# Seven block products in place of eight in a graph layer's polynomial, with an order of issue found by a search

## The chip, the cores and the metric

The kernel runs on one core of a Trainium2 chip. The metric is the device time of one execution in microseconds (us); the number used is the median of the runs. The engines are named as in the profile: PE does matrix products, PEld is its loading of the stationary operand, DVE is the vector engine, ACT the scalar engine, POOL is GpSimd, and SP issues every DMA of this kernel.

## The reference

64 graphs of 256 nodes with 128 features each go through four layers, every one with a residual sum and a layer norm over the features. All graphs share one weighted adjacency matrix A (256 x 256). The first layer is a gated recurrent update that runs five times; it makes most of the products. The second and third are convolution and attention layers. The last layer, which is the one changed, takes three powers of the adjacency over two copies of the same graph:

```
h1 = A @ x;  h2 = A @ h1;  h3 = A @ h2                    # per graph
y  = x@v0 + h1@v1 + h2@v2 + h3@v3 + h1@v4 + h2@v5 + h3@v6  # v: 128 x 128
out = layernorm(x + y)
```

With `q = A x` this is `P + A^2 R`, where `P = x (v0 + I) + q (v1 + v4)` and `R = x (v2 + v5) + q (v3 + v6)`. The weights are centred beforehand, so that the norm has no mean to subtract.

## The kernel before, in words

Two graphs make a pair, and the 32 pairs go through the layers independently of one another, several at a time. All data are 32-bit floats, and a tile is 128 partitions by 512 columns: 2 graphs x 2 blocks of 128 nodes x 128 features.

No engine's order is written by hand. Each piece of work is recorded as an `Op` by `S.add` with the engines that it could run on, an assumed duration for each, and what it reads and writes. When all is recorded, `Schedule.order` (L132) plans: it takes, again and again, the operation that can start earliest by its assumed durations, with the more urgent one first where two can start together (`due`, L128, and what remains of the pair behind it). It also chooses the engine where there is a choice, and a buffer of the class that the value belongs to (`CLASSES`, L41: 30 buffers of class `A` in SBUF, 8 of `PS`, the PSUM banks). The planned starts then give the order in which each engine's instructions are issued. On the chip each engine follows its list in that order and waits wherever an operand or a buffer isn't ready.

Names that matter below: `mm` (L59) is the assumed duration of a product; `MARGIN` makes the assumed durations of all engines but PE 10% longer; `SEEN` and `LAG` are the assumed time until another engine can use a result. `evacuate` (L234) copies from PSUM to SBUF, on ACT or on DVE; its records have the lines 236 and 237. `turn` (L514) transposes a tile: a transpose of 32 x 32 blocks on DVE (L529), one DMA to DRAM (L531), four DMAs back (L537). `spread7` (L553, products at L566) multiplies by an adjacency matrix with seven block products, `spread` (L548) with eight. `products` (L721) multiplies by one or two 128 x 128 matrices. `scale_norm` (L672) takes the mean square on ACT (L645) or DVE, its root on POOL (L650, L653), and scales on ACT or DVE (L665, L667).

`layer3` (L814) of a pair takes `xT`, the turned tile, and `qT = (A x)^T`. Its eight products (L827, L828), each 256 columns wide, give P and R of both graphs at once; R is copied to SBUF (`rr`, two copies of 256 columns), and four products of 256 columns with `a2T` (L835) add A² R to P in PSUM:

```
pr = t.at(2, 2, D)[:, :, b, :]
nc.tensor.matmul(pr, tokens(xT)[:, c, :], vx.ap, start=(b == 0), stop=False, skip_group_check=True)
nc.tensor.matmul(pr, tokens(qT)[:, c, :], vq.ap, start=False, stop=(b == 1), skip_group_check=True)
```

Of the kernel before, what the change touches and what calls it, by code (L numbers as in the profile page):

```python
# [12 lines left out]
P = 128  # L13
N = 256
# [9 lines left out]
SEVEN = {"q1": 4, "g": 4, "q3": 4}  # L24
FIRST, FINAL = 2, 0

# [14 lines left out]
CLASSES = {"X": (512, 15), "T": (512, 4), "A": (512, 30), "H": (520, 6), "B": (1024, 6), "S": (32, 64), "PS": (512, 8), "D": (512, 4), "E": (1024, 8)}  # L41
# [15 lines left out]


def mm(cols):  # L59

    return cols * 0.00168 + 0.005


class Value:
# [3 lines left out]
    def __init__(self, cls=None, ap=None, name="v"):  # L68
        self.cls, self.ap, self.name = cls, ap, name
        self.writers, self.readers, self.left, self.end = [], [], 0, 0.0  # L70


        self.seeded = self.full = False
# [21 lines left out]
class Op:  # L95
    def __init__(self, pair, ways, reads, writes, number, dma):
        self.pair, self.ways, self.reads, self.writes, self.number, self.dma = pair, ways, reads, writes, number, dma
        self.seen = LAG + (sum(dma) if dma else SEEN[ways[0][0].rstrip("+-")])
        self.before, self.then, self.waits, self.ready, self.rest = {}, [], 0, 0.0, 0.0


class Schedule:
# [29 lines left out]
    def order(self, tiles):  # L132
        for op in self.ops:
            op.waits = len(op.before)
            for b in op.before:
                b.then.append(op)
            for v in op.holds:
                v.left += 1
        for op in reversed(self.ops):
            us = min(w[1] for w in op.ways) + op.seen  # L140
            op.rest = us + max((x.rest for x in op.then if x.pair == op.pair), default=0.0)
        free = {cls: [(0.0, t) for t in ts] for cls, ts in tiles.items()}
        full = {}
        engines = dict.fromkeys([*SEEN, "PORT"], 0.0)
        ready = [op for op in self.ops if not op.waits]
        out, moved = [], 0.0
        while ready:
            best = None
            for op in ready:
                held = 0.0  # L150
                for v in op.holds:
                    if v.cls and v.ap is None:
                        held = max(held, min((t for t, a in free[v.cls] if full.get(id(a)) or not v.seeded), default=1e9))
                if held == 1e9:
                    continue
                way = None
                for engine, us, fn in op.ways:
                    us = us if engine == "PE" else us * MARGIN
                    start = max(op.ready, held, *(engines[e] for e in USES.get(engine, (engine,))))
                    end = start + us + SPARE.get(engine, 0.0)  # L160
                    if way is None or end < way[0]:
                        way = end, start, op, engine, us, fn
                late = self.due(op.pair) - op.rest + HOLD[op.layer] if op.pair >= 0 else -1e4
                key = (way[1], late, op.number)
                if best is None or key < best[0]:
                    best = key, *way[1:]
            if best is None:
                raise RuntimeError("no operation can start: too few tiles")
            _, start, op, engine, us, fn = best
            ready.remove(op)  # L170
            for v in op.holds:
                if v.cls and v.ap is None:
                    slot = min((s for s in free[v.cls] if full.get(id(s[1])) or not v.seeded), key=lambda s: s[0])
                    free[v.cls].remove(slot)
                    v.ap = slot[1]
            end = start + us
            engines.update(dict.fromkeys(USES.get(engine, (engine,)), end))
            if op.dma:
                wait, move, seen = op.dma
                moved = max(moved, end + wait) + move * MARGIN  # L180
                op.seen = moved + seen - end + LAG
            out.append((start, op.number, op, fn))
            for v in op.holds:
                v.left -= 1
                v.end = max(v.end, end + op.seen)
                if not v.left and v.cls:
                    free[v.cls].append((v.end, v.ap))
                    full[id(v.ap)] = v.full or v.seeded
            for x in op.then:
                x.waits -= 1  # L190
                same = engine != "SP" and x.ways[0][0].rstrip("+-") == engine.rstrip("+-")
                x.ready = max(x.ready, end + (AGAIN.get(engine.rstrip("+-"), 0.0) if same else op.seen))
                if not x.waits:
                    ready.append(x)

            op.tiles = {v: v.ap for v in op.holds}
        assert len(out) == len(self.ops), "operations that wait for one another"
        self.span = max(engines.values())
        return [(op, fn) for _, _, op, fn in sorted(out, key=lambda x: x[:2])]


@with_exitstack
def kernel(ctx: ExitStack, tc: tile.TileContext, x, xT, adj, adjT, mats, cols, rows, out):
# [11 lines left out]
    def pe(us, fn, r, w):  # L215
        S.add([("PE", us, fn)], r, w)
# [4 lines left out]
    def dve(us, fn, r, w):  # L221
        S.add([("DVE", us, fn)], r, w)
# [144 lines left out]
    pe(mm(256), edge_cols, [rowb, numb], [t1])  # L367
# [20 lines left out]
    pe(mm(1024), edge_values, [erow, colk], [t3])  # L388
# [70 lines left out]
    pe(mm(1024), square, [a, aT], [t7])  # L459
# [17 lines left out]
    centre(vq, lambda: vq.ap, 2)  # L477

# [24 lines left out]
    def tokens(v):  # L503
        return v.at(4, D)
# [37 lines left out]
    def spread(i, right):  # L542

        t = bank()
        for b in range(2):
# [4 lines left out]
            pe(mm(512), fn, [i, right, *[t] * b], [t])  # L550
# [126 lines left out]
    def layer0(x0, hT):  # L677
        h = x0
        for s in range(STEPS):
# [6 lines left out]
            pe(mm(1024), reset, [Wg, w4, hT, mT], [t])  # L686
# [14 lines left out]
            pe(mm(1024), candidate, [w5, u5h, mT, r], [t])  # L701
# [13 lines left out]
    def products(lefts, rights, t=None):  # L715

        first, t = t is None, t or bank()
        for c in range(4):
# [4 lines left out]
            pe(mm(128 * len(lefts)), fn, [*lefts, W1, *[t] * bool(c or not first)], [t])  # L723
        return t

    def layer1(x1):
        qT = spread7(x1, offT, offT7) if S.pair < n_pairs - SEVEN["q1"] else to_sbuf(spread(x1, offT), "qT")
# [14 lines left out]
    def layer2(x2):  # L742
# [3 lines left out]
        for b in range(2):  # L746
# [5 lines left out]
            pe(mm(260), fn, [xT, wpx], [t])  # L752
# [34 lines left out]
        for b in range(2):  # L787
# [6 lines left out]
            pe(mm(512), fn, [wT, h, *[t] * b], [t])  # L794
# [18 lines left out]

    def layer3(x3, p):  # L814
        xT = turn(x3, "xT", "x3")
        qT = spread7(x3, aT, aT7) if S.pair < n_pairs - SEVEN["q3"] else to_sbuf(spread(x3, aT), "qT")

        rr, o = Value("A", name="rr"), Value("A", name="o")
        ts = []
        for i in range(2):  # L820
# [8 lines left out]
            pe(mm(1024), fn, [xT, qT, vx, vq], [t])  # L829
            evacuate(lambda i=i: rr.at(2, N)[:, i], lambda t=t: t.at(512)[:, N:], [t], [rr], (0.28, 0.34))  # L830
            ts.append(t)
        for i, t in enumerate(ts):
# [4 lines left out]
            pe(mm(512), fn, [a2T, rr, t], [t])  # L837
        s, rs = scale_stats([(t, range(i, 4, 2)) for i, t in enumerate(ts)])
        for i, t in enumerate(ts):
            scale_tokens(t, o, range(i, 4, 2), s, rs)  # L840
        S.add([("SP", 0.4, lambda: nc.sync.dma_start(out[2 * p:2 * p + 2].rearrange("b (t p) d -> p (b t) d", p=P), tokens(o)))],
              [o], [], (0.6, 1.0, 0.9))
# [14 lines left out]
    with tc.manual_schedule():  # L857
        for op, fn in S.order(tiles):
            for v, ap in op.tiles.items():
                v.ap = ap  # L860
            fn()
# [40 lines left out]
```

## Time and profile before

| | us |
|---|---|
| median of three runs | 1489.29 |
| lowest and highest run | 1488.52, 1491.57 |
| span of the profiled execution, first to last instruction | 1485.2 |
| median less span (launch and end, and what differs from run to run) | 4.1 |
| PE busy | 1474.5 (99% of the span) |
| DVE busy | 1234.4 (83%) |
| ACT busy | 1026.9 (69%) |
| POOL busy | 829.8 (56%) |
| weight loads busy | 1062.6 (72%) |
| share of the DMA queue's packets of 16 engines' span | 70.7% |

The device time of the profiled execution is not given apart; its span is what the sums are made against, and the 4.1 us are put on top. A record's duration on PE overlaps with the next record's, so the row of PE's busy time only says where PE had nothing at all. A 32-bit product leaves two records of PE in the profile (7704 records are 3852 products).

### The profile page before, as it was taken

The numbers are of one execution on the slowest core, as the hardware profiler recorded it, in microseconds if no ns is written. First come the engines' busy times: TensorE is split into PE (matmuls) and PEld (weight loads), VectorE is DVE, ScalarE is ACT, GpSimd is POOL, SyncE is SP. The second block draws the span as 40 slices with busy tenths as digits, with TensorE's granted clock in tenths as the row PEclk, the third lists the DMA queues.
The fourth block names the chain that finished last, engine by engine and source line by source line (L and its number), as shares of the span: only waits on it lengthen the run. The fifth ranks groups of instructions, "written<-read, shape, count | busy, mean of one in ns | idle before, by whom it ended". The sixth has DMA issues, their size and how long they took to land.

```text
span 1485.2 us, 28119 instructions
## 1 busy us (share of the span) xinstructions
PE 1474.5 (99%) x7704; PEld 1062.6 (72%) x7704; DVE 1234.4 (83%) x3083; ACT 1026.9 (69%) x3116; POOL 829.8 (56%) x1307
## 2 busy tenths in 40 slices
PE   9999999999999999999999999999999999999998
PEld 6556666666676677777767777777676776788997
DVE  7767888988999899888888888878888888989872
ACT  3444556667777787876776767676686767878875
POOL 4412434555576776564556556565454746676542
PEclk9999999999999999999999999999999999999999
DMA  8544565777788978776778668777777776667762
GB/s 239 121 85 99 104 131 121 144 148 152 156 156 173 176 167 171 161 160 135 148 148 178 134 134 174 155 158 143 142 166 148 151 153 124 136 136 148 165 123 71
DMA packets 946845, 216.60 MB, mean 146 GB/s; under 512 B 726017, under 2 KB 942209, under 8 KB 946689
## 3 DMA queue, kind: packets, MB, share of 16 engines
q1 hardware_dynamic: 946688, 214.81, 70.7%
q8 instruction: 62, 1.02, 0.3%
q14 instruction: 95, 0.77, 0.2%
HBM read 116.86 MB, written 97.85 MB: 145 GB/s over the span
## 4 chain that ended last, share of the span: by engine, by line
PE 95%; DVE 2%; DMA 1%; ACT 0%; issue 0%; SPq 0%; POOL 0%; POOLq 0%; ACTq 0%; DVEq 0%
PE ps L566 23%; PE ps L699 9%; PE ps L700 9%; PE ps L684 9%; PE ps L685 9%; PE ps L692 9%; PE ps L721 7%; PE ps L835 4%; PE ps L828 4%; PE ps L827 4%; PE ps L791 4%; PE ps L548 2%; PE ps L751 2%; DMA x<-x_in 1%; DMA a<-e 0%; DVE a L529 0%
## 5 line engine op out<-in xcount | busy, mean ns | idle before, releaser
L566 PEld LDWEIGHTS ps<-aT,a 128*128 128x128 f32 x2144 | 291.4, 192 | 83.3 <-issue 76.7
L236 ACT COPY a<-ps 128x128 f32<-128x128 f32 (+2 forms) x553 | 230.4, 433 | 137.8 <-PE ps L566 48.6
L566 PE MATMUL ps<-aT,a 128*128 128x128 f32 x2144 | 315.7, 275 | 0.9 <-DMA a<-e 0.5
L585 POOL TENSOR_TENSOR a<-a 128x128 f32<-128x128 f32 x205 | 103.7, 510 | 150.4 <-DVE a L581 110.6
L688 ACT ACTIVATE a<-ps,bzrh 128x512 f32<-128x512 f32 x160 | 110.0, 688 | 104.4 <-PE ps L685 90.7
L703 ACT ACTIVATE ps<-ps,bzrh 128x512 f32<-128x512 f32 x160 | 106.1, 663 | 105.3 <-PE ps L700 102.3
L699 PE MATMUL ps<-a,w 128*128 128x512 f32 x320 | 163.7, 593 | 0.0
L685 PE MATMUL ps<-a,w 128*128 128x512 f32 x320 | 163.4, 592 | 0.0
L700 PE MATMUL ps<-a,u5h 128*128 128x512 f32 x320 | 163.4, 592 | 0.0
L692 PE MATMUL ps<-a,w 128*128 128x512 f32 x320 | 162.8, 593 | 0.0
L645 ACT ACTIVATE a<-ps 128x128 f32<-128x128 f32 x488 | 128.7, 282 | 45.9 <-PE ps L721 20.9
L529 DVE STREAM_TRANSPOSE a<-a 128x512 f32<-128x512 f32 x215 | 149.7, 700 | 10.9 <-DMA e<-a 2.2
L587 DVE TENSOR_TENSOR a<-ps,a 128x256 f32<-128x256 f32 x234 | 96.5, 416 | 67.8 <-ACT a L236 32.0
L721 PE MATMUL ps<-W,a 128*128 128x128 f32 x1024 | 144.5, 275 | 0.0
L721 PEld LDWEIGHTS ps<-W,a 128*128 128x128 f32 x1024 | 132.8, 192 | 16.1 <-issue 13.9
L653 POOL TENSOR_TENSOR s<-s,neg_half 128x4 f32<-128x4 f32 x128 | 138.1, 1079 | 7.6
L694 ACT ACTIVATE a<-ps,bzrh 128x512 f32<-128x512 f32 x160 | 110.5, 691 | 45.2 <-PE ps L692 37.8
L684 PE MATMUL ps<-a,W 128*128 128x512 f32 x256 | 131.0, 593 | 0.0
L685 PEld LDWEIGHTS ps<-a,w 128*128 128x128 f32 x320 | 60.8, 190 | 76.5 <-issue 68.1
L700 PEld LDWEIGHTS ps<-a,u5h 128*128 128x128 f32 x320 | 60.8, 190 | 76.5 <-issue 64.8
L705 DVE SCALAR_TENSOR_TENSOR ps<-a,ps 128x512 f32<-128x512 f32 x160 | 109.7, 686 | 6.1 <-ACT a L694 4.4
L573 POOL TENSOR_TENSOR a<-a,a 128x128 f32<-128x128 f32 x133 | 67.3, 507 | 83.6 <-DVE a L572 55.3
(208 smaller groups left out, 3329.2 us busy)
## 6 DMA issues: line engine op xcount, KB each, us to landing
e<-a SPq DMA_DIRECT2D x277, 256.0 KB
a<-e SPq DMA_DIRECT2D x1108, 64.0 KB
e<-b SPq DMA_DIRECT2D x32, 512.0 KB
b<-e SPq DMA_DIRECT2D x128, 128.0 KB
x<-x_in SPq DMA_DIRECT2D x32, 256.0 KB
t<-xT_in SPq DMA_DIRECT2D x32, 256.0 KB
a<-d SPq DMA_DIRECT2D x32, 256.0 KB
y_out<-a SPq DMA_DIRECT2D x32, 256.0 KB
```

Source lines behind the costliest of these rows:

```text
L236: S.add([("ACT", us[0], lambda: nc.scalar.copy(o(), i())), ("DVE", us[1], lambda: nc.vector.tensor_copy(o(), i()))], r, w)
L529: dve(n / 512 * 0.55 + 0.09, lambda: nc.vector.transpose(st.at(n), i.at(n)), [i], [st])
L566: pe(mm(128), lambda: nc.tensor.matmul(blk(t, k), left(), rt(), start=start, stop=True, skip_group_check=True), [*r, right, terms, *[t] * ...
L645: nc.scalar.activation(tokens(junk)[:, c, :], v.at(len(tiles), D)[:, k, :], AF.Square, scale=D ** -0.5, accum_out=mv()[:, c, 1:2])
L653: pool(1.02, lambda: nc.gpsimd.tensor_tensor(rs(), rs(), neg_half.ap, op=ALU.pow), [s, neg_half], [s])
L684: nc.tensor.matmul(t.at(512), mat("u3"), hT.at(512), start=True, stop=False)
L685: nc.tensor.matmul(t.at(512), w4.ap, mT.at(512), start=False, stop=True)
L692: pe(mm(512), lambda t=t, mT=mT: nc.tensor.matmul(t.at(512), w3.ap, mT.at(512), start=False, stop=True, skip_group_check=True), [w3, mT, t ...
L694: act(0.59, lambda t=t, z=z: nc.scalar.activation(z.at(512), t.at(512), AF.Tanh, bias=bzrh.ap[:, 0:1], scale=0.5), [t, bzrh], [z])
L699: nc.tensor.matmul(t.at(512), w5.ap, mT.at(512), start=True, stop=False)
L700: nc.tensor.matmul(t.at(512), u5h.ap, r.at(512), start=False, stop=True)
L721: nc.tensor.matmul(tokens(t)[:, c, :], tokens(i)[:, c, :], w(), start=(first and k == c == 0), stop=(k == len(lefts) - 1), skip_group_chec ...
```

## The change

1. **Layer 3 of pairs 0 to 29.** With the two graphs as rows and x, q as columns, P and R are a 2 x 2 block product: `[[x0, q0], [x1, q1]]` by `[[vx0, vx1], [vq0, vq1]]`. `polynomial7` makes it from seven block products of 2 x 128 columns, with sums of operands ahead of them (on DVE or POOL) and sums of results behind them (on DVE, out of PSUM), as Strassen's scheme in Winograd's form does. The sums of weights (`vt`) are made once, at the start. The last two pairs keep the old form.
2. **The planner.** `order` now keeps up to four plans at a time. Every 60 us of planned time each is continued eight times, once as it is and seven times with the urgency of each operation moved by up to 2 us at random (from a fixed seed); the four with the least idle time of PE are kept, where idle time is counted by a second reckoning that follows each engine in its order with the assumed durations but without the 10%, plus 0.3 of the idle time in the plan itself.
3. **Assumed durations and buffers.** `mm` counts products one by one (0.2241 us for up to 130 columns), and class `A` has 38 buffers. `layer1b` is another form of the second layer; with `L1 = -1` no pair takes it.

```diff
-SEVEN = {"q1": 4, "g": 4, "q3": 4}
+SEVEN = {"q1": 4, "g": 4, "q3": 4, "pr": 2}
+L1 = -1
...
-CLASSES = {"X": (512, 15), "T": (512, 4), "A": (512, 30), ...
+CLASSES = {"X": (512, 15), "T": (512, 4), "A": (512, 38), ...
...
+SOON = {"PE": 0.2, "ACT": 0.17, "DVE": 0.15, "POOL": 0.15, "SP": 0.0}
+WINDOW, TRIES, KEPT, NUDGE, IDLE = 60.0, 8, 4, 2.0, 0.3
-def mm(cols):
-    return cols * 0.00168 + 0.005
+def mm(cols, n=1):
+    return n * (0.2241 if cols <= 130 else cols * 0.001665 + 0.0065)
...
+                late = op.late
+                if seed and op.pair >= 0:
+                    late += NUDGE * ((op.number * 7919 + seed * 104729) * 2654435761 % 4294967296 / 2147483648.0 - 1.0)
                 key = (way[1], late, op.number)
...
+        tracks, until, seed = [self.prepare(tiles)], 0.0, 0
+        while any(t.ready for t in tracks):
+            until += WINDOW
+            found = []
+            for t in tracks:
+                for k in range(TRIES if t.ready else 1):
+                    c = t.copy()
+                    seed += 1
+                    self.run(c, until, seed * bool(k))
+                    found.append(c)
+            tracks = sorted(found, key=lambda t: t.real_idle + IDLE * t.idle)[:KEPT]
+        best = min((t for t in tracks if t.number == len(self.ops)), key=lambda t: t.end)
...
+    vt = fixed([4, D], "vt")
+    for k, (left, right) in enumerate(((lambda: vx.ap[:, 1, :], lambda: vx.ap[:, 0, :]),
+                                       (lambda: vq.ap[:, 1, :], lambda: vt.ap[:, 0, :]),
+                                       (lambda: vq.ap[:, 1, :], lambda: vx.ap[:, 1, :]),
+                                       (lambda: vq.ap[:, 0, :], lambda: vt.ap[:, 1, :]))):
+        dve(0.25, lambda k=k, left=left, right=right: nc.vector.tensor_sub(vt.ap[:, k, :], left(), right()), [vx, vq, vt], [vt])
...
     def layer3(x3, p):
         xT = turn(x3, "xT", "x3")
         qT = spread7(x3, aT, aT7) if S.pair < n_pairs - SEVEN["q3"] else to_sbuf(spread(x3, aT), "qT")
+        if S.pair < n_pairs - SEVEN["pr"]:
+            return polynomial7(xT, qT, p)
...
+    def polynomial7(xT, qT, p):
+
+        half = lambda v, k: v.at(2, N)[:, k]
+        s13, s24, sv, rr, o = (Value("A", name=n) for n in ("s13", "s24", "sv", "rr", "o"))
+        s1, s3, s2, s4 = Part(s13), Part(s13), Part(s24), Part(s24)
...
+        sum_(0.335, 0.8, lambda e: e.tensor_sub(S3(), x0(), x1()), [xT], [s3])
+        sum_(0.335, 0.8, lambda e: e.tensor_sub(S2(), q1(), S3()), [qT, s3], [s2])
+        sum_(0.335, 0.8, lambda e: e.tensor_add(S1(), x1(), q1()), [xT, qT], [s1])
+        sum_(0.335, 0.8, lambda e: e.tensor_sub(S4(), q0(), S2()), [qT, s2], [s4])
+
+        y, t = bank(), Value("PS", name="ps")
+
+        def product(v, k, left, right, r, start=False):
+            def fn():
+                for i in range(2):
+                    nc.tensor.matmul(tokens(v)[:, 2 * k + i, :], left()[:, i * P:(i + 1) * P], right(), start=start and i == 0,
+                                     stop=True, skip_group_check=True)
+            pe(mm(128, 2), fn, [*r, vx, vq, vt, *[v] * (not start)], [v])
...
+        product(y, 0, x0, VX(0), [xT, s2], start=True)
+        product(y, 1, S2, VT(1), [s2])
+        product(t, 0, S1, VT(0), [s1], start=True)
+        evacuate(lambda: half(sv, 0), lambda: half(y, 0), [y], [sv], (0.28, 0.335))
+        dve(0.335, lambda: nc.vector.tensor_add(half(y, 1), half(y, 1), half(sv, 0)), [y, sv], [y])
+        evacuate(lambda: half(sv, 1), lambda: half(y, 1), [y], [sv], (0.28, 0.335))
+        product(y, 1, S3, VT(2), [s3])
+        product(y, 0, q0, VQ(0), [qT])
+        evacuate(lambda: half(sv, 0), lambda: half(y, 1), [y], [sv], (0.28, 0.335))
+        product(y, 1, q1, VT(3), [qT])
+        dve(0.335, lambda: nc.vector.tensor_add(R(1), blocks(t, 0), blocks(sv, 0)), [t, sv], [rr])
+        product(t, 0, S4, VQ(1), [s4])
+        dve(0.335, lambda: nc.vector.tensor_add(R(0), blocks(t, 0), blocks(sv, 1)), [t, sv], [rr])
+        for i in range(2):
+            def fn(i=i):
+                for j in range(2):
+                    nc.tensor.matmul(y.at(2, 2, D)[:, :, i, :], a2T.ap[:, j, i * P:(i + 1) * P], rr.at(2, 2, D)[:, j],
+                                     start=False, stop=(j == 1), skip_group_check=True)
+            pe(mm(256, 2), fn, [a2T, rr, y], [y])
+        scale_norm(y, o)
+        store(o, p)
```

The products of the new form are named below by what stands on their left: x0, S2 and S1 first, then S3 and q0, then q1 and S4, then the four with `a2T`. Because the planner decides anew, hardly any instruction keeps its place: the built order differs from the first few dozen products on.

## The prediction

> **What bounds the kernel now.** I read the page first (busy time, clock, the chain that ended last).
>
> ```profile
> span 1485.2 us, 28119 instructions
> PE 1474.5 (99%) x7704; PEld 1062.6 (72%) x7704; DVE 1234.4 (83%) x3083; ACT 1026.9 (69%) x3116; POOL 829.8 (56%) x1307
> ...
> PEclk9999999999999999999999999999999999999999
> ...
> PE 95%; DVE 2%; DMA 1%; ACT 0%; issue 0%; SPq 0%; POOL 0%; POOLq 0%; ACTq 0%; DVEq 0%
> ```
>
> PE lacks work for 10.7 us of 1485.2, the clock is full, and the chain is 95% PE. A busy row alone proves little, since its records overlap; so next the chain in order of time around 710 us (start, us, what), which shows the pace at which PE gets through products:
>
> ```profile
> 709.82 1.34 PE ps L566 x12
> 711.16 0.45 PE ps L751 x4
> 711.61 0.22 PE ps L566 x2
> 711.83 0.89 PE ps L791 x8
> ...
> 715.14 0.43 PE ps L827 x2
> 715.58 0.43 PE ps L828 x2
> 716.01 0.43 PE ps L827 x2
> 716.44 0.43 PE ps L828 x2
> 716.87 0.67 PE ps L566 x6
> ```
>
> Two records are one product. One of 128 columns takes 1.34/6 = 0.2235 us, whatever its line; four of 256 take 716.87 - 715.14 = 1.73, so 0.4325 each. There is no gap: PE is fed at its own pace. Where it isn't, stretches of the span tell (from:to, length, PE busy and the others):
>
> ```profile
> 0.00:50.00 50.00, 48.59 (x190) 31.07 (x191) 37.31 (x94) 19.73 (x33) 28.03 (x54) 1.00 0.84 220
> 50.00:450.00 400.00, 400.00 (x1860) 257.93 (x1859) 333.41 (x728) 248.24 (x633) 183.58 (x296) 1.00 0.64 128
> 450.00:500.00 50.00, 47.94 (x272) 34.32 (x271) 45.22 (x118) 36.37 (x109) 33.84 (x53) 1.00 0.93 177
> 500.00:1000.00 500.00, 500.00 (x2698) 364.60 (x2699) 425.70 (x1074) 366.84 (x1140) 306.10 (x483) 1.00 0.76 156
> 1000.00:1360.00 360.00, 360.00 (x1985) 267.89 (x1984) 312.58 (x809) 263.52 (x833) 217.87 (x338) 1.00 0.72 145
> 1360.00:1400.00 40.00, 39.01 (x269) 36.19 (x269) 37.21 (x130) 34.82 (x139) 26.73 (x36) 1.00 0.78 160
> 1400.00:1485.00 85.00, 78.93 (x442) 70.56 (x440) 42.93 (x136) 57.34 (x234) 33.62 (x51) 0.99 0.51 106
> ```
>
> The start loses 1.4 us, 450 to 500 loses 2.06 (DMA share 0.93; PE waits for an input tile, a turned tile and a copy), 1360 to 1400 loses 0.99 (on DVE's sum of the second residual), and nothing elsewhere until the end, where 6 us follow the last product: square, root, scaling, store.
>
> [...] the products at L566 have a mean record of 275 ns while records start 112 ns apart. [...] two narrow products cost 0.447 against 0.4325 for a wide one. [...]
>
> **The change part by part**, against the profiled span.
>
> *Products.* Per pair, 8 of 256 columns go (8 x 0.4325 = 3.46) and 14 of 128 come (14 x 0.2235 = 3.13). The products with `a2T` stay four of 256. 30 x 0.33 = **-9.9 us**, all on the path. With PE saturated, work taken from it shortens the span unless something else makes PE wait.
>
> *Side work.* In the built order DVE gets 90 more sums out of PSUM (x 0.416, L587) and 57 of the 120 operand sums (x 0.434); 63 go to POOL (x 0.746). ACT makes 29 more copies of 256 columns (x 0.376, L236). The planner in turn gives POOL 17 of DVE's 512-wide operations (0.7 us each) and ACT 16 of its scalings. So DVE +38 us (about 86%), ACT +24 (71%), POOL +68 (61%). Cost nothing, hidden under PE, as long as each result is early enough. The four sums for `vt` (4 x 0.28 on DVE at the start) lie hundreds of us ahead of their use. No DMA is added or taken away.
>
> *New hand-offs.* Here PE could come to wait. From the tail, where the last `qT` was late: PE's product ends, 0.26 us later ACT begins its copy, and PE goes on 0.05 after it. So q1, which needs a copy after S3 and q0, needs 0.26 + 0.38 + 0.05 = 0.69 us; S3, behind copy, sum and copy, 0.26 + 0.38 + 0.1 + 0.42 + 0.1 + 0.38 + 0.05 = 1.7; `a2T`, behind S4 and a sum, 0.73. I laid the built PE order out at the paces above. The PE work that lies between: before q1 at least 1.12 us, median 2.2, with six pairs under 1.4; before S3 at least 2.45, median 6; before `a2T` 1.3 or more, but for pair 23 (0.45) and pair 29 (none). So only pair 23 waits (0.3 us), and pair 29 (0.73, in the tail). An ACT operation of 0.69 us caught in front of q1's copy would use up the smallest spares.
>
> *The order elsewhere.* The plan is chosen by PE's reckoned idle time, so the two stalls of the middle (3.05 us) may go; their kind (DMA crowding, late sums near the end) may come back elsewhere, and 8 more buffers of class `A` don't speed any transfer. I take two thirds, **-2.0 us**; the bounds are -3.05 (nothing lost) and +6, twice as much again as now.
>
> *The tail.* The last residual tile must be normed and turned before the last pair's products. Before:
>
> ```profile
> 1464.81 0.37 SPq L531 DMA_DIRECT2D e<-a  x1
> 1467.16 1.92 SPq L537 DMA_DIRECT2D a<-e  x4
> ```
>
> The last product of layer 2 (L721) ended at about 1459.4, SP issued the first leg at 1464.81, and the second leg from 1467.16; it has landed at about 1470.6, if the last of its four takes about the 1.5 us (estimate, from the 2.35 of the four times larger first leg). That is 11.2 us, and 13.6 us of products covered it. In the new order there lie between the last L721 product and the use: two block products (0.89), four `a2T` (1.73), eight of the old form (3.46), four L548 (1.73), four old `a2T` (1.73): 9.55 us. The wait is about 1.7 us, pair 29's inside it; DVE and SP have nothing late in front. Before, the tail lost 0.3 there to a copy that the new order covers: **+1.4**. The old form's last pair and what follows its last product stay.
>
> Sum: -9.9 - 2.0 + 0.3 + 1.4 = -10.2, span 1475.0, and with the 4.1 us between span and median **1479.1**.
>
> **The rivals.**
>
> *A, as summed*: 1479.1, own range 1475.5 to 1482. For it: PE without a gap over 1260 us, distances longer than the hand-offs. Chance 0.68.
>
> *B, small waits at the new hand-offs*, or DMA crowding as at 450 to 500: if each copy or sum stands behind one 0.69 us activation, q1 needs 1.38 and S3 3.8; against the distances, pair by pair, this costs 0.5 + 2.6 us; with the middle's stalls unchanged (+2.0) the time is 1484. For it: ACT and DVE are above 70% and issue strictly in order. Against: the old form's copies stood under the same load and PE waited 0.3 us in all for them. Chance 0.20.
>
> *C, slower: DVE or ACT becomes the bound of layer 3.* Hand-offs repeat three times per pair where there was one. If every link stands behind two activations (1.4 us), q1 needs 2.1 and S3 5.9 us; summed over the pairs' distances 6 + 21 = 27 us, so 1506. It turns the sign once waits eat 10.2 us, 0.34 per pair, and is measurably slower at 0.44. Against it: DVE would stand at 86% and has slack in every stretch (426 of 500). Chance 0.05.
>
> *D, the change doesn't take work from PE*: were the narrow products paced at 0.247 us or more (3.46/14), the gain would be nil, and the time 1489.3 - 2.0 + 1.7 = 1489. L566, L721 and L791 all show 0.2235 at such lengths. Chance 0.02. The remaining 0.05 is for an order so much better (all stalls and the tail's wait gone: 1485.2 - 9.9 - 3.4 + 4.1 = 1476, or less where the row hid stalls) or a disturbed figure.
>
> **How the numbers follow.** The prediction is A's. The range 1475 to 1484.5 holds A, the better order's upper half and most of B: a little over 8 in 10. A measurement of this kernel tells 0.2% (3 us) from no change. Faster by more (under 1486.3): A, nine tenths of B, and nearly all of the better order, 0.88. Within: the rest of B, D and the upper foot of A, 0.07. Slower: C, 0.05.
>
> **What would show it.** PE's records rise to 8064 (180 more products, but narrow ones), while PE's busy time falls with the span to about 1464.5, at 99%; the block products start 0.22 us apart. DVE rises to about 86%, ACT to 71%, POOL to 61%. In the list of PE's waits a line for `xT` coming back by DMA, 1 to 2 us, stands at about 1460 us, or the wait on DVE's sum just ahead of it. Wrong would be: PE waits for ACT's copies or DVE's sums inside layer 3 of over 3 us in total (B or C), stretches of the middle with PE below 99% (another order's stalls), or block products further apart than 0.23 us (D).

## The result, and the profile after

The changed kernel takes 1486.14 us (median of four runs, 1485.48 to 1486.72), beside 1488.90 for the kernel before (four runs): a ratio of 0.9986, interval 0.9971 to 1.0001. A later comparison, with twelve runs of the changed kernel, gave 0.9996 (0.9987 to 1.0004). So the change moves the time by nothing that can be told, where 10 us were forecast, and the figure lies outside the forecast's range.

The page of the kernel after, with the shares of the chain that ended last:

```profile
span 1484.7 us, 28833 instructions
PE 1468.3 (99%) x8064; PEld 1066.6 (72%) x8064; DVE 1270.5 (86%) x3182; ACT 1044.6 (70%) x3185; POOL 899.5 (61%) x1383
...
PE 92%; DVE 5%; DMA 1%; ACT 1%; issue 1%; SPq 0%; POOL 0%; POOLq 0%; ACTq 0%; DVEq 0%
```

The counts and shares are the forecast ones to a point: 8064 records, DVE 86%, ACT 70, POOL 61. But PE was busy for 1468.3 us where 1464.5 were expected, and DVE's part of the chain went from 2% to 5%. The stretches of the kernel after (from:to, length, then busy time of PE, weight loads, DVE, ACT, POOL with their records, PE's granted clock, DMA share, GB/s), cut as before:

```profile
0.00:50.00 50.00, 48.80 (x200) 32.15 (x201) 40.17 (x99) 20.68 (x34) 26.52 (x52) 1.00 0.78 209
50.00:450.00 400.00, 400.00 (x1843) 256.56 (x1842) 332.30 (x725) 247.75 (x617) 193.00 (x307) 1.00 0.65 130
450.00:500.00 50.00, 49.60 (x316) 38.79 (x315) 46.05 (x129) 39.87 (x134) 34.93 (x57) 1.00 0.85 169
500.00:1000.00 500.00, 496.99 (x2792) 362.05 (x2791) 441.51 (x1105) 369.17 (x1141) 328.83 (x505) 1.00 0.77 155
1000.00:1360.00 360.00, 359.54 (x2119) 271.65 (x2118) 321.14 (x844) 274.14 (x886) 246.58 (x369) 1.00 0.75 149
1360.00:1400.00 40.00, 38.64 (x310) 37.20 (x309) 37.59 (x130) 34.48 (x136) 33.06 (x47) 1.00 0.71 147
1400.00:1485.00 85.00, 74.74 (x495) 68.18 (x494) 51.77 (x156) 58.51 (x242) 36.58 (x51) 0.99 0.47 100
```

PE lacks 3.0 us between 500 and 1000 (before: nothing), and in the last 85 us it is busy for 74.74 where it was busy for 78.93, though the span is only half a microsecond shorter. PE's list of waits (in us: total, times, longest) names them:

```profile
PE ps L660 <- DMA x<-x_in: 2.5, 1, 2.5
PE ps L1017 <- DVE a L1013: 1.9, 2, 1.5
...
PE ps L994 <- DVE a L1011: 1.0, 1, 1.0
...
PE ps L957 <- DMA a<-e: 0.2, 1, 0.2
```

The first is for an input tile, at 500 us. The next two are for the new sums of results (L1011, L1013), all after 1400 us, and the last is for the turned tile of the last pair. There is no line of L994 behind a copy on ACT.

**One reckoning for all runs.** Busy time hides what is lost when records overlap (a record of L994 lasts 275 ns in the mean, and the next starts 112 ns after it), so I added up PE's records by their starts. At PE's own pace records lie 112, 216 or 429 ns apart, by width (128, 256, 512 columns); the sum of that is the *pace*, and what a start lies later than its pace is *lost*. Every profiled span is, within 0.1 us, 1.2 (before the first product) + pace + lost + 6.3 (behind the last one's start; 6.6 without the search and 6.8 with DVE handicapped). Before: 1.2 + 1470.8 + 6.9 + 6.3 = 1485.2. After: 1.2 + 1461.2 + 16.0 + 6.3 = 1484.7. PE's work fell by 9.6 us, and lost time rose by 9.1.

| kernel | median us | ratio to before | pace | lost | to 450 | 450-560 | 560-1300 | 1300-1425 | then |
|---|---|---|---|---|---|---|---|---|---|
| before | 1486.5-1488.9 | 1 | 1470.8 | 6.9 | 1.7 | 3.3 | -0.6 | 1.7 | 0.8 |
| after | 1486.14 | 0.9986 | 1461.2 | 16.0 | 1.8 | 5.8 | -0.3 | 5.9 | 2.8 |
| after, again | 1486.28 | 0.9996 | 1461.2 | 13.6 | 1.7 | 3.6 | -0.4 | 6.1 | 2.7 |
| no search | 1491.55 | 1.0031 | 1461.2 | 21.6 | 2.6 | 7.6 | 2.2 | 7.0 | 2.2 |
| old products | 1485.74 | 0.9993 | 1470.8 | 4.5 | 2.6 | -0.1 | -0.2 | 2.0 | 0.2 |
| other seed | 1485.22 | 0.9990 | 1461.2 | 18.2 | 2.1 | 2.4 | -0.4 | 11.1 | 3.1 |
| no sums of results | 1482.60 | 0.9977 | 1461.2 | 14.1 | 2.6 | 5.5 | -0.2 | 3.5 | 2.7 |
| no sums of operands | 1482.00 | 0.9970 | 1461.2 | 10.7 | 2.4 | 2.2 | -0.8 | 4.0 | 2.8 |
| no sums | 1480.60 | 0.9961 | 1461.2 | 10.5 | 2.4 | 2.9 | -1.0 | 3.4 | 2.8 |
| load only | 1494.34 | 1.0048 | 1470.8 | 14.7 | 2.8 | 5.3 | 1.1 | 5.3 | 0.3 |
| last 12 pairs old | 1486.21 | 1.0000 | 1464.4 | 10.2 | 2.3 | 3.1 | 0.7 | 3.4 | 0.7 |
| new form in pairs 20-29 only | 1486.06 | 0.9994 | 1467.6 | 11.6 | 1.7 | 1.9 | -0.2 | 5.6 | 2.6 |
| 17 input buffers | 1489.30 | 1.0022 | 1461.2 | 16.5 | 1.8 | -0.1 | 1.3 | 10.8 | 2.7 |
| layer 3 sooner | 1506.43 | 1.0131 | 1461.2 | 37.0 | 2.1 | 0.6 | 4.6 | 12.2 | 17.5 |
| operand sums on POOL | 1490.46 | 1.0024 | 1461.2 | 18.5 | 1.9 | 3.0 | 1.5 | 9.2 | 2.9 |
| the same, last 12 pairs old | 1485.27 | 0.9990 | 1464.4 | 13.0 | 2.0 | 3.4 | 4.7 | 2.7 | 0.2 |
| DVE handicapped | 1495.13 | 1.0064 | 1461.2 | 24.1 | 3.9 | 1.2 | -0.4 | 15.0 | 4.5 |
| DVE handicapped, last 12 pairs old | 1492.16 | 1.0042 | 1464.4 | 17.8 | 3.7 | 1.5 | 0.9 | 10.8 | 1.0 |
| 17 input buffers, last 12 old | 1488.88 | 1.0016 | 1464.4 | 16.9 | 2.7 | -0.1 | 0.0 | 12.1 | 2.2 |
| the same, other seed | 1483.75 | 0.9981 | 1464.4 | 10.7 | 2.3 | 0.2 | -0.5 | 6.8 | 2.0 |

The lost columns are of one profiled execution each (two for the changed kernel, which differ by 2.2 us at 450 to 560). The medians are of several, so the two agree to 2 or 3 us only. The profiles of the other seed (1488.63 us) and of the new form in pairs 20 to 29 (1488.59) are the slowest of twelve runs, that of the last 12 pairs old (1483.86) is the fastest of twelve: their lost time stands 3.4 and 2.5 us too high, and 2.4 too low. The lost time also holds stretches at half of the full clock (last section). In "after" it is one of 3.4 us, at 500 us, which cost 1.7 us, and the mean granted clock of the profiled execution is 0.998. It is 0.998 without the search too, with the other seed (0.97 from 1375 to 1400 us, 0.96 from 1400 to 1425), without the sums of results (0.98 from 450 to 560) and in the second row with DVE handicapped: an estimated one stretch each, as 1.7 us are 0.001 of the span. It is 0.997 in the first of these rows (0.93 from 1350 to 1400) and in the first of the last two rows (0.93 from 1300 to 1350), an estimated two, 0.996 in "layer 3 sooner", an estimated three, and 0.999 or 1.000 in all others. In every later comparison the time of before was 1486.5 to 1486.7, and the ratio is the number to compare by.

### The profile page after: what moved, and what is told of

The parts are those of the page before. It is cut to its first block, busy times and chain, and to the rows that moved or that the text cites. A ratio compares the mean times of both kernels' runs of the same rounds, so it can differ in the third digit from the quotient of the medians.

```text
span 1484.7 us, 28833 instructions
## 1 busy us (share of the span) xinstructions
PE 1468.3 (99%) x8064; PEld 1066.6 (72%) x8064; DVE 1270.5 (86%) x3182; ACT 1044.6 (70%) x3185; POOL 899.5 (61%) x1383
## 3 DMA queue, kind: packets, MB, share of 16 engines
q1 hardware_dynamic: 946688, 214.81, 71.4%
## 4 chain that ended last, share of the span: by engine, by line
PE 92%; DVE 5%; DMA 1%; ACT 1%; issue 1%; SPq 0%; POOL 0%; POOLq 0%; ACTq 0%; DVEq 0%
PE ps L660 23%; PE ps L778 9%; PE ps L779 9%; PE ps L786 9%; PE ps L793 9%; PE ps L794 9%; PE ps L815 7%; PE ps L994 5%; PE ps L915 4%; PE ps L1017 3%; PE ps L642 2%; PE ps L875 2%; DMA x<-x_in 1%; DVE a L623 0%; DVE x L711 0%
## 5 line engine op out<-in xcount | busy, mean ns | idle before, releaser
L324 ACT COPY a<-ps 128x512 f32<-128x512 f32 (+2 forms) x588 | 243.0, 433 | 112.7 <-PE ps L660 41.3
L815 PEld LDWEIGHTS ps<-W,a 128*128 128x128 f32 x1024 | 131.4, 192 | 15.7 <-issue 13.6
L675 POOL TENSOR_TENSOR a<-a 128x256 f32<-128x256 f32 x114 | 84.9, 746 | 88.2 <-ACT a L324 85.9
```

The lines of the kernel that those rows point to most:

```text
L324: S.add([("ACT", us[0], lambda: nc.scalar.copy(o(), i())), ("DVE", us[1], lambda: nc.vector.tensor_copy(o(), i()))], r, w)
L815: nc.tensor.matmul(tokens(t)[:, c, :], tokens(i)[:, c, :], w(), start=(first and k == c == 0), stop=(k == len(lefts) - 1), skip_group_chec ...
```

## The experiments

All edits are to the changed kernel, and "the search" is the planner's. Only the three runs that leave sums out keep PE's order. Every other run but the repeat has an order of its own, and two orders of the same work differ by up to 5.1 us (the last two rows), which is more than most differences below. Theory D is throughout that the load of the side work, on DVE above all, gives the saving back; its rivals are told in the expectations that name them.

### The two halves of the change apart

```diff
-WINDOW, TRIES, KEPT, NUDGE, IDLE = 60.0, 8, 4, 2.0, 0.3
+WINDOW, TRIES, KEPT, NUDGE, IDLE = 60.0, 1, 1, 2.0, 0.3     # no search
...
-SEVEN = {"q1": 4, "g": 4, "q3": 4, "pr": 2}
+SEVEN = {"q1": 4, "g": 4, "q3": 4, "pr": 32}                # old products
...
-        tracks, until, seed = [self.prepare(tiles)], 0.0, 0
+        tracks, until, seed = [self.prepare(tiles)], 0.0, 5000   # other seed
```

> The changed kernel with the planner's search taken out (one plan, one continuation, no nudges); seven products, new assumed durations and 38 buffers stay. Theory 1 (the new hand-offs cost time where few pairs are left, at the end): PE loses 5 to 7 us beyond its pace after 1360 us as in the changed kernel, with waits on the sums of layer 3; time 1486 to 1490. Theory 2 (the stalls belong to the one order that the search found): the end loses 2 us or less, and the time is 1480 to 1484.

> The search, the assumed durations and the buffers of the change, but layer 3 with eight products in all 32 pairs. Theory 1: the end's losses fall back to about 2 us as before the change; the middle's stall at the first reloaded input may stay; time 1487 to 1490 (before's, less what the search wins). Theory 2: losses at the end of 5 us or more although no new hand-off is there; time 1492 or more.

> The changed kernel with another start of the random numbers in the search: another order of the same work. Theory 1: the same time to 1 us (1485 to 1487), and 5 us or more lost after 1360 us. Theory 2: a time that differs by 3 us or more in either direction, the losses at other places.

> The changed kernel again, unaltered, so that it stands beside the others on their chip. Both theories: 2 to 3 us under the kernel before.

Measured: without the search the new products are slower than before, 1.0031 (1.0018 to 1.0044). The search with the old products is at 0.9993 (0.9984 to 1.0002): it removes 2.4 us of lost time (3.4 at 450 to 560, less 1 elsewhere), about what I had forecast for it. Another seed gives 0.9990 (0.9982 to 0.9999), with 11.1 us lost at 1300 to 1425. So neither half, nor both, brings what the fewer products save; and the loss moves with the order. The expectations missed in size: without the search the time is above the 1486 to 1490 us of theory 1, with the old products it is below its 1487 to 1490, and the changed kernel was 0.2 us under the kernel before, not 2 to 3.

### Taking the side work away, the order kept

```diff
-        dve(0.335, lambda: nc.vector.tensor_add(half(y, 1), half(y, 1), half(sv, 0)), [y, sv], [y])
+        dve(0.335, lambda: None, [y, sv], [y])     # and so the sums into R(1), R(0): no sums of results
...
-            S.add([("DVE+", us, lambda: fn(nc.vector)), ("POOL", us_pool, lambda: fn(nc.gpsimd))], r, w)
+            S.add([("DVE+", us, lambda: None), ("POOL", us_pool, lambda: None)], r, w)   # no sums of operands
```

> The changed kernel with its order kept, but the three sums out of PSUM of each pair's seven products are not issued (left out: the additions that combine the block products, so layer 3 is not computed). Leaves DVE 37 us and breaks the hand-offs that go over it. Theory D (DVE is full from 1300 to 1425 us and the sums stand in its queue) and theory L (the hand-offs are long whatever the load) both expect 4 to 5 us less than the changed kernel, with the waits on the sums of layer 3 gone.

> The changed kernel with its order kept, but the four sums of operands ahead of each pair's products are not issued (left out: the sums of x and q blocks, so layer 3 is not computed). Takes 25 us from DVE and 47 from POOL and leaves the hand-offs behind the products as they are. Theory D: DVE has room between 1300 and 1425 us, the waits there shrink by half or more, 2 to 4 us less. Theory L: under 1 us less.

> The order of the changed kernel, with all seven sums of the new form left out (four of operands, three of results; their place in each queue and what waits for what stays, but the work isn't done, and its output isn't the reference's); the copies stay. The two halves of this gave 1482.0 and 1482.6. Load and length of the sums both gone: if sums explain what is returned, the loss after 1300 us falls from 8.7 to the 2 to 4 us of the old form, and the time to 1479 to 1481. If the copies and the mere order of the products do it, it stays at 1482 or above.

Measured: 0.9977 (0.9971 to 0.9984) without the sums of results, 0.9970 (0.9960 to 0.9980) without those of operands, 0.9961 (0.9946 to 0.9976) without either. PE's instructions and their order are those of the changed kernel, so these three are free of the luck of an order. Against the changed kernel's later comparison (0.9996) the sums cost 0.35%, 5.2 us; those of operands alone 0.26%, 3.9 us, although PE was shown to wait for none of them. Part of that lies at 500 us: without the operand sums the wait for the input tile there is 0.9 us (1.0 with no sums at all), in place of 2.5 and 2.0 in the two executions of the changed kernel. Why it is shorter is not shown. The stretches of the kernel with no sums at all, columns as above:

```profile
560.00:1300.00 740.00, 740.00 (x4217) 544.16 (x4216) 627.78 (x1585) 547.50 (x1707) 454.52 (x702) 1.00 0.75 151
1300.00:1425.00 125.00, 122.89 (x900) 111.72 (x899) 106.19 (x338) 109.88 (x421) 85.70 (x121) 1.00 0.78 153
```

and the same two of the changed kernel:

```profile
560.00:1300.00 740.00, 739.94 (x4202) 542.79 (x4201) 654.20 (x1664) 547.48 (x1700) 482.06 (x738) 1.00 0.75 151
1300.00:1425.00 125.00, 121.30 (x885) 109.74 (x884) 117.78 (x366) 109.41 (x416) 97.05 (x138) 1.00 0.75 148
```

In the middle DVE does 26 us more with the sums, and PE lacks 0.06: there they cost nothing, as forecast. At 1300 to 1425 DVE does 11.6 us more, is busy for 117.78 of 125, and PE lacks 1.6 us more (2.5 by the starts); most of the rest lies at 450 to 560. With no sums at all 6.2 us are still lost after 1300, where the expectation had 2 to 4, so the sums explain the loss there only in part. What these runs take away is both the load on the engines and the lateness of the results (the products with `a2T` wait for no sum any more, unlike what the expectation says); the next run has the load alone, in an order of its own.

### The side work alone

```diff
     def layer3(x3, p):
...
-        if S.pair < n_pairs - SEVEN["pr"]:
+        if False:
             return polynomial7(xT, qT, p)
...
+        if S.pair < n_pairs - SEVEN["pr"]:
+            side_work(xT, qT, ts)   # four sums of xT, qT; three of ts with them, one copy; read by nobody
```

> All pairs multiply in the old form, but pairs 0 to 29 also do the new form's side work for nobody: four operand sums on DVE or POOL, three sums of 256 columns out of PSUM on DVE, one copy. No product waits for any of it, and PE's products are those of the kernel before (with the search's order). Theory D (the load itself returns the gain): 5 to 7 us of PE's time are lost in the drain beyond the run with the old products and the search, 1491 to 1493. Theory H (the chain of hand-offs is what PE waits for): within 2 us of that run's 1485.7.

Measured: 1.0048 (1.0033 to 1.0063), against 0.9993 with the same products and no such work: 0.55%, 8.2 us. The expectation had 5 to 7 us more lost in the drain; 3.4 more are lost after 1300, and 5.4 more at 450 to 560. Two stretches of it:

```profile
450.00:560.00 110.00, 106.20 (x582) 76.58 (x581) 95.96 (x256) 82.16 (x259) 80.18 (x123) 1.00 0.82 165
...
1300.00:1425.00 125.00, 121.38 (x764) 105.33 (x762) 111.84 (x347) 108.27 (x411) 85.52 (x128) 1.00 0.73 143
```

and of the search with the old products:

```profile
450.00:560.00 110.00, 110.00 (x609) 79.64 (x608) 97.41 (x254) 84.58 (x260) 81.06 (x125) 1.00 0.85 171
...
1300.00:1425.00 125.00, 123.27 (x807) 109.66 (x806) 107.92 (x340) 106.23 (x413) 80.81 (x116) 1.00 0.76 152
```

With work whose results no product reads PE loses more, at the same two places as in the changed kernel. Theory H, that PE waits for the chain of new hand-offs, needs nothing of that kind to happen. The size is less sure than the sign: this kernel has an order of its own, its side work also holds buffers, and two orders of the same work have differed by 5.1 us (the last pair of runs).

### Where it is lost

```diff
-SEVEN = {"q1": 4, "g": 4, "q3": 4, "pr": 2}
+SEVEN = {"q1": 4, "g": 4, "q3": 4, "pr": 12}                # last 12 pairs old
...
-        if S.pair < n_pairs - SEVEN["pr"]:
+        if n_pairs - 12 <= S.pair < n_pairs - SEVEN["pr"]:  # new form in pairs 20 to 29 only
...
-CLASSES = {"X": (512, 15), "T": (512, 4), "A": (512, 38), ...
+CLASSES = {"X": (512, 17), "T": (512, 4), "A": (512, 37), ...   # 17 input buffers
...
-HOLD = (0.0, -20.0, 0.0, 40.0)
+HOLD = (0.0, -20.0, 0.0, 0.0)                               # layer 3 sooner
```

> The changed kernel with the old form of layer 3 in the last 12 pairs in place of the last 2. PE's work rises by 10 x 0.33 = 3.3 us. Theory 1: the waits on the sums of layer 3 after 1360 us go, 4 to 5 us less, so 1484 to 1485.5, no slower than the changed kernel. Theory 2: 3.3 us slower, about 1489.5.

> The new form in pairs 20 to 29 only, the old one in the others: PE has 10 x 0.33 = 3.3 us less to do than before, and all new hand-offs lie in the drain. If the drain is where the gain is returned: 5 to 7 us more lost after 1300 us than with the old products, so slower than the run with the old products and the search by 1 to 4 us, 1487 to 1490. If it is lost anywhere: 3 us faster than that run, 1482 to 1483.

> The changed kernel with 17 buffers for the inputs in place of 15 and 37 of class A in place of 38, so that the 16th pair's input need not wait until the first pair's is released. If the stall at 500 us (2.6 us of waiting and about 2 us of slow products after it) comes from that, it is gone from there, or comes two pairs later if loads are late there as well; without it the time is 3 to 5 us under the changed kernel, unless a new order loses it again at the end.

> The 40 us by which the planner counts layer 3 as less urgent become 0, so that layer 3 of a pair is issued sooner; by the built order about 8 pairs instead of 12 run their layer 3 in the last 150 us of products. All 30 pairs have the new form. If the crowding of layer 3 at the end is the cause, the loss after 1300 us falls by about a third or more (3 us or more) and the time goes to 1483 or below. If not: within 2 us of 1486; if layer 3 had served to fill gaps in the drain, slower.

Why the end matters is seen in the records of the new products (L994, 28 in each of 30 pairs) of the changed kernel, by stretch (from:to, length, PE busy with them, clock, DMA share, GB/s):

```profile
0.00:1300.00 1300.00, 73.07 (x500) 1.00 0.73 149
1300.00:1485.00 185.00, 44.81 (x340) 1.00 0.63 126
```

340 of 840 records, 12 of 30 pairs, lie in the last 185 us, an eighth of the span. The planner counts layer 3 as less urgent, so it piles up there, with all that the new form puts on DVE, ACT and POOL.

With the old form in the last 12 pairs the loss after 1300 us falls from 8.7 to 4.1 us, and PE has 3.2 us more to do; the ratio is 1.0000 (0.9991 to 1.0008). With the new form in pairs 20 to 29 alone it is 0.9994 (0.9986 to 1.0003), the same as with old products throughout, and 8.2 us are lost after 1300, against 2.2. My expectation of 1 to 4 us slower was too high; but the 3.2 us saved did not come out either. In this one order, work taken from PE in the drain was not time taken from the kernel.

17 input buffers take away the stall at 500 (lost at 450 to 560: none), and 13.5 us are lost after 1300 instead: 1.0022 (1.0014 to 1.0030). Layer 3 issued sooner is far slower, 1.0131 (1.0114 to 1.0148). Its waits:

```profile
PE ps L815 <- ACT ps L324: 3.3, 5, 1.6
PE ps L994 <- DVE a L1011: 3.1, 3, 2.1
...
PE ps L957 <- DMA a<-e: 2.4, 1, 2.4
```

and 17.5 us lost after 1425. This fits that the layer 3 products held back are the work with which PE covers the last pairs' chain of turns, norms and copies. Little was moved: 550 of the 840 records of L994 start before 1300 us, in place of 500. So issuing layer 3 sooner does not help; whether the crowding does harm beside this is not told apart. That each block product saved in the drain is cover saved too is argued, not measured.

### Relieving DVE, and both places at once

```diff
-            S.add([("DVE+", us, lambda: fn(nc.vector)), ("POOL", us_pool, lambda: fn(nc.gpsimd))], r, w)
+            S.add([("POOL", us_pool, lambda: fn(nc.gpsimd))], r, w)   # operand sums on POOL
...
-SPARE = {"DVE": 1.0, "DVE+": 0.0, "POOL": -0.3}
+SPARE = {"DVE": 1.6, "DVE+": 0.4, "POOL": -0.3}                      # DVE handicapped
```

> The four operand sums of the new form may run on POOL only, so DVE is rid of some 57 sums of 0.43 us (25 us, 1.7% of the span) and POOL gets them at 0.75 us; the planner orders everything anew. Theory D, that the gain comes back as waits because DVE is full in the drain from 1300 us on: DVE's busy share falls from 86% to about 84%, the time PE has nothing in 1300 to 1425 us falls, and the time falls by 2 to 4 us. Rival P, that what the products save is lost to any new order whatever DVE's load (late input tiles, a planner that doesn't reckon with queues): within 2 us of the changed kernel, with waits of another kind. A further rival, that POOL's slower sums are late themselves: PE waits for POOL's sums of layer 3, and it is slower.

> As the run before, and the last 12 pairs keep the old form, so that the drain has neither its sums nor its hand-offs; PE has 10 x 0.33 = 3.3 us more to do. Theory D: the drain loses no more than the kernel before did (about 2 us between 1300 and 1425 us), so that 20 x 0.33 = 6.6 us of saving remains but for what the stretch around 500 us loses: 1480 to 1484. Rival P: near 1486 like the changed kernel with the last 12 pairs in the old form.

> The planner's handicap on DVE goes from 1.0 to 1.6 us for what reads PSUM, and from 0 to 0.4 us for the rest, so that some 270 operations fewer go to DVE, and most of them to POOL; DVE's share falls from 86% to an estimated 79%, POOL's rises to about 71%. The computation is the same. Theory D: the waits on DVE's results in the drain go, the time falls by 3 us or more, to 1483 or less. Rival P: no change beyond 2 us. If operations of 0.7 us and more on POOL come too late, slower.

Measured: 1.0024 (1.0015 to 1.0034), 0.9990 (0.9982 to 0.9998) and 1.0064 (1.0050 to 1.0078). Theory D had all three faster by 2 us or more, and two are slower. No wait for an operand sum on POOL is in the first one's list, so that these come late themselves is not seen. The row of busy times of the kernel with the handicap on DVE:

```profile
PE 1473.1 (99%) x8064; PEld 1070.2 (72%) x8064; DVE 1199.6 (80%) x2899; ACT 1070.1 (72%) x3270; POOL 1071.2 (72%) x1626
```

its drain, columns of the stretches as above:

```profile
1300.00:1425.00 125.00, 116.87 (x818) 104.54 (x816) 111.89 (x331) 106.04 (x402) 97.23 (x140) 0.97 0.69 138
```

and the head of PE's waits:

```profile
PE ps L660 <- DVE a L666: 2.6, 1, 2.6
PE ps L660 <- POOL a L667: 1.8, 1, 1.8
```

DVE's share went down as planned, and in the drain it has the load of the kernel before (111.89 us against 111.45), yet 15.0 us are lost there. So "DVE is full" is not the whole cause. POOL took what DVE gave up, at 746 ns for a sum that takes DVE 432 (L675, in the changed kernel), and PE now waits for scalings on POOL too. What is left is weaker, and fits these waits without being shown apart: side work on engines that work in the order of their lists, on any of the three, makes results late where few pairs are left to cover for them. That order is seen in the trace of the changed kernel: 3054 instructions of DVE, 2558 of ACT and 1383 of POOL stand in it as in the kernel's lists.

One more run had the handicap on DVE and the old form in the last 12 pairs. Theory D expected it to be slower than with the handicap alone, by up to 3.3 us, and took the opposite for a sign that the new hand-offs in the drain cost something of their own. It was 3.0 us faster, 1492.16 us, 1.0042 (1.0029 to 1.0055). But it does not compute the reference's output, for a cause that was not found, so it carries little weight.

The last two runs took both places away at once, 17 input buffers and the old form in the last 12 pairs, with two seeds.

> 17 input buffers in place of 15 (and 37 of class A in place of 38), which took away the stall at 500 us in an earlier run, and the old form in the last 12 pairs, which brought the loss in the drain down to 3 to 4 us. If these two places are all: PE's work 1464.4 by its pace, about 6 us lost in all, 1.2 before the first product and 6.3 behind the last one, and 1.8 from span to time: 1480, 0.4% faster than before. If every order loses its 10 us or more somewhere whatever is relieved: 1484 to 1487.

> The same with the search's other starting number, so another order of the same work. If the two places are the cause, within 2 us of the run before it; if the luck of one order makes the difference, further apart.

Measured: 1.0016 (1.0009 to 1.0023) and 0.9981 (0.9974 to 0.9987), 1488.88 and 1483.75 us: the first slower than before, the second 2.7 us faster than before on the same chip and the fastest complete kernel here. The stall at 500 is gone in both, and 14.3 and 8.8 us are lost after 1300, where 3 to 4 had been hoped for. The expectation of 1480 failed; and two orders of the same work lie 5.1 us apart, so the gain of the better one can't be put down to the two edits. In the profiles, an estimated 3.5 us of the difference are the clock of the slower one, 0.93 in the 50 us from 1300 to 1350; waits of 3.1 and 2.0 us stand in its list, and none over 1.2 us in that of the faster one.

## Why the prediction was wrong, step by step

**Products, -9.9: right as PE's work, not as time.** The pace fell by 9.6 us. The chain in order of time (start, us, what) shows that block products run at 0.22:

```profile
706.11 0.86 PE ps L786 x2
706.97 0.45 PE ps L994 x4
707.41 0.86 PE ps L786 x2
```

Rival D, narrow products paced too slowly, is out. The sentence behind it, "with PE saturated, work taken from it shortens the span", holds only where PE is saturated. It was applied to all 30 pairs, though 12 of them run layer 3 in the drain. Of the 9.6 us about half came out even with no sums at all: 0.9961 against 0.9993 for the old products with the search, 4.8 us.

**Side work at no cost: the step that failed.** "DVE has slack in every stretch (426 of 500)" was read off the wide stretches, as if the +38 us were spread evenly; the prediction's own rows for 450 to 500 and 1360 to 1400 us had DVE at 45.22 of 50 and 37.21 of 40. Two fifths of layer 3 run in the last eighth, which the counts by line of the old products showed before the change as well (112 of 256 records of L827 after 1300 us). At 1300 to 1425 us DVE was at 111.45 of 125 before, and is at 117.78 after (shown above). The kernel before:

```profile
1300.00:1425.00 125.00, 124.01 (x803) 110.10 (x802) 111.45 (x340) 102.14 (x397) 82.70 (x119) 1.00 0.75 152
```

What that does is seen on DVE's queue at 1413 us (start, us, instruction, idle before it in brackets):

```profile
1413.24 0.86 DVE L694 BATCH_NORM_STATS2 s<-a 128x6 f32<-128x128 f32 x4
1414.03 0.35 DVE L696 BATCH_NORM_AGGREGATE s<-s 128x2 f32<-128x6 f32 x4
1414.31 0.38 DVE L1011 TENSOR_TENSOR a<-ps,a 128x256 f32<-128x256 f32 x1
```

and PE's, at the same time:

```profile
1413.36 0.39 PE L660 MATMUL ps<-aT,a 128*128 128x128 f32 x2
1414.75 0.71 PE L994 MATMUL ps<-vq,a 128*128 128x128 f32 x4 [1.00 <-DVE a L1011]
```

DVE has no gap at all; the sum stands 1.1 us behind the statistics of a norm, and S4's product stands 1.00 us. With the sums left out and the order kept the kernel is 5.2 us faster: that is the term set at nothing. It is a little over half of what went wrong. The forecast had 6.6 us lost and 16.0 were, 9.4 too many; with no sums 10.5 are still lost. What takes these other 4 us no experiment shows.

**Hand-offs, +0.3: right for the copies, with one link left out.** PE shows no wait for the copies ahead of S3 and q1. (The 0.1 us put in for each hand-off between ACT and DVE was my estimate; in the kernel before, L529 on DVE starts at 1464.07 us, 0.03 behind the end of ACT's L622, for which it waited.) S4 was not among the links priced, though its product adds onto the block that the sum of L1011 must have read first; this is the wait of 1.0 us above. It and the 0.4 of `a2T` for L1013 outside the tail are of sums behind other pairs' work on DVE, which the 0.26 + 0.42 of an idle engine left out. This is rival B's mechanism, with DVE in ACT's place. The sign named for it, over 3 us of such waits, just failed to show: 2.9 us, 1.45 of them in the tail.

**The order elsewhere, -2.0: right for the search, wrong for the whole.** The search with the old products removes 2.4 us. With the new products 450 to 560 loses 5.8 (3.6 in the other execution) against 3.3 before. The chain at that place:

```profile
497.66 0.91 PE ps L778 x2
498.57 4.50 DMA x<-x_in
503.06 0.14 issue
503.20 0.46 PE ps L660 x2
503.66 1.54 PE ps L778 x2
505.20 1.71 PE ps L779 x2
506.90 1.03 PE ps L786 x2
```

SP issued the input tile's load at 498.57, right behind eight DMAs of 4.19 us in all (L631), and PE stood for 2.47 us. The stall depends on the order and on the buffers (none with the old products or with 17 input buffers); in the load-only run 5.3 us are lost in this stretch. The packets of SP's DMA queue took 71.4% of 16 engines' span, where the same 214.81 MB took 70.7% before: the added buffers sped no transfer.

**The tail, +1.4: about right.** 2.0 more are lost after 1425. The wait was 1.45 on DVE's last sum (L1013, behind the norm of the last tile) with 0.2 for the turned tile behind it, where I had 1.7 with the sum inside it. The copy that I had taken as covered by the new order cost 0.5 (L965), in place of 0.3.

**4.1 us from span to median: mis-sized.** The time of a profiled execution is 1.8 us above its span in the runs of the changed kernel (1486.49 and 1484.7). If so before too, its profiled execution took 1487.0, near the 1486.5 of the later comparisons: the three runs around 1489 would be at the slow end. With 1.8 the forecast would have been 1476.8, further off.

The sum closes: 1475.0 + 0.3 (products) + 16.0 - 6.6 (lost: forecast 6.9 - 2.0 + 0.3 + 1.4) = 1484.7.

What stays open is what decides within an order. The savings of the first 20 pairs, 6.4 us by pace, did not come out in any of the four complete runs that had them alone: against the search with the old products (0.9993) the best of them gains 0.12%, 1.8 us, and the losses are found at 450 to 560, in the middle, or after 1300, depending on the order. Nor was it tried to shorten the drain's own chain, the turns and norms of the last pairs.

## What to carry to other kernels

Before pricing side work at nothing, count where it runs: take the line's records by stretch and compare the extra load with the slack of that stretch, not of the whole. At the end of a pipeline, work on the busiest engine may also be cover for everybody else's latency; here products saved there brought nothing that could be told, and issuing them sooner made the kernel 1.3% slower. And where a planner lays out everything anew, run two seeds before reading a gain of a few tenths of a per cent as that of an edit.

## What the runs showed of the hardware

After the 2.47 us wait PE ran at a lower clock. The stretches around it:

```profile
499.00:503.00 4.00, 1.73 (x6) 0.60 (x4) 3.19 (x7) 3.35 (x12) 0.81 (x2) 1.00 0.83 158
503.00:508.00 5.00, 4.80 (x9) 2.25 (x10) 3.25 (x9) 1.53 (x3) 4.70 (x7) 0.66 0.91 210
508.00:513.00 5.00, 5.00 (x25) 3.12 (x24) 3.71 (x6) 4.39 (x11) 3.42 (x5) 1.00 0.64 101
```

The granted clock is 0.66 from 503 to 508 (1.00 up to 503.7, 0.50 from there to 507.1), and pairs of 512-column records take 1.54, 1.71 and 1.03 us (the chain above) where they take 0.86 otherwise: 1.7 us on top of the wait. So this stall cost two thirds more than the list of waits shows.

In the other execution of the same kernel PE stood for 1.99 us at this place, and the clock stayed, at 1.00 and 0.98:

```profile
499.00:503.00 4.00, 2.01 (x8) 0.90 (x7) 3.21 (x7) 3.33 (x12) 1.16 (x3) 1.00 0.75 149
503.00:508.00 5.00, 5.00 (x19) 2.61 (x18) 3.72 (x10) 3.56 (x7) 4.78 (x8) 1.00 0.98 218
```

So of the 2.2 us between the two executions at 450 to 560, 0.5 are the wait and 1.7 the clock. The length of a single wait does not tell whether the clock falls: with the other seed the longest in PE's list after 1300 us is 1.8 us, and the clock is 0.97 from 1375 to 1400 us and 0.96 from 1400 to 1425. What does tell was not shown.

The operand sums on POOL took 770 to 901 ns in the mean of a line (L984 to L987), where I had taken 746 from the sums of the kernel before; on DVE the same sums took 419 to 508.
